# Squaring the queries and keys behind their two rotary products instead of ahead of them

## The chip, the cores and the metric

The kernel runs on one core of one Trainium2 chip. The metric is the device time of one execution in microseconds (us). An engine's name here is the profile's: PE is TensorE (with PEld for its weight loads), DVE is VectorE, ACT is ScalarE, POOL is GpSimd, SP is SyncE, which only issues transfers. SBUF is the on-chip working memory; PSUM is the small memory, in banks of 128 partitions x 512 fp32 numbers, that PE writes its results to and that DVE and ACT read.

## The reference, cut to what matters

The input has 4 sequences of 2048 tokens and 256 channels. A full attention of 16 heads comes first; behind it stand two local layers, and the change lies in these. One local layer computes, for 8 heads of 64:

```python
qkv = h @ wqkv
q, k, v = jnp.split(qkv, 3, axis=-1)
q = l2norm(q) * qs            # t / clip(norm(t), 1e-12), by head
k = l2norm(k) * ksc
q, k = rotary_xpos(q, k)      # q * cos * scale + rotate_half(q) * sin * scale; k with 1 / scale
o = local_attention(q, k, v)  # windows of 128 tokens, each sees itself and the one before
x = x + o @ wo
h = layernorm(shift_token(x)) * lg + lb
a, g = jnp.split(h @ w1 + b1, 2, axis=-1)
x = x + (a * gelu(g)) @ w2 + b2
```

The norm of a query or key is one number by token and head, so it commutes with the rotation. The kernel therefore rotates the raw product and multiplies by the reciprocal norm later.

## The kernel before, in words

The attention comes first and is not touched. The local layers follow: 2 layers x 4 sequences x 16 windows of 128 tokens are 128 steps, each called by its layer, sequence and window (l, b, c). Four steps share one feed-forward block, so the pattern of the work repeats every four steps; c mod 4 names the place in it.

One step runs through these pieces, each on one engine. `project` (from L1408) turns the tokens (`ht`), and `product` (L1434) multiplies them on PE with the three weight tiles into three banks `qkv`, taken from a pool of two banks. For queries (i = 0) and keys (i = 1), `scale` (L1444) reads the finished bank three times: ACT squares it into `sq` (L1454), and DVE multiplies it with two rotary tables into `r` and `t` (L1456). `square_sum` (L1460) sums `sq` by head into `ss` on DVE, and `rotate` (L1465) adds the shifted `t` to `r` on POOL (L1469). `unit` (L1481 to L1491) makes the reciprocal norm: DVE bounds `ss` from below (L380), POOL raises it to the power of minus a half (L381, tile `rn`), DVE scales the eight numbers of the queries (L1487, tile `rn8`) and multiplies the keys by theirs (L1488). For the queries the reciprocal norm enters the exponent later.

`attend` transposes `r` on PE (`qt`, `kt`, L1508), splits each result into a high part on ACT (`lq` L1513, `lk` L1522) and a low part on DVE (L1406, a helper), moves the keys' halves across partitions by DMA (L1528), multiplies (`sim`, L1544), adds the mask and takes the row maximum on DVE (L1556, L1562), exponentiates on ACT (L1570), takes the reciprocal of the sums on DVE (`inv`, L1578) and multiplies by it on POOL (L1581). `gather` transposes these weights on PE (`pT`, L1603), copies them out on ACT and DVE (L1614), weighs the values (`po`, L1624), multiplies with `wo` (`lo`) and adds to the residual (`fg`, L1654). `glu` does the feed-forward block of four steps: the shift by DMA (`shg`), statistics (L391 to L396), normalisation (`hn`, L1689), its transposes (`hnt`, L1704), and the two products, all of whose matmuls stand on L421.

Two things set the order of the work. A timetable written out by hand (`AT`) puts the pieces into slots, and so sets the order in which the instructions are given. A list scheduler then orders each engine's queue by its own estimate of durations and waits. An engine executes its queue strictly in that order. The scheduler also keeps any two engines from touching one PSUM bank at the same time, reads too, in the order in which the two instructions were given: before, DVE's products wait for ACT's square of the same bank.

Of the kernel before, what the change touches and what calls it, by code (L numbers as in the profile page):

```python
# [31 lines left out]
AF = mybir.ActivationFunctionType  # L32
# [160 lines left out]
def encoder_kernel(  # L193
# [22 lines left out]
    nc = tc.nc  # L216
# [161 lines left out]
    def inverse_root(dst, var, least, op):  # L378

        nc.vector.tensor_scalar(var, var, least, None, op)  # L380
        nc.gpsimd.tensor_tensor(dst, var, nhalf[:, : var.shape[1]], ALU.pow)  # L381
# [37 lines left out]
    def dense(*args, **kwargs):  # L419
        for product in dense_products(*args, **kwargs):  # L420
            product()  # L421
# [912 lines left out]
    def local_layers():  # L1334
        with ExitStack() as es:
# [11 lines left out]
            def psum(name):  # L1347

                banks = pq if name.startswith("qkv_") else pp
                return banks.tile([P, 512], F32, tag="ps", name=name)  # L1350
# [23 lines left out]
            def put(at, key, pieces):  # L1374

                assert len(pieces) == len(AT[key]), key
                for slot, piece in zip(AT[key], pieces):
                    tt.put(at + slot, piece)

            def each(f, n):  # L1380
                return [partial(f, i) for i in range(n)]
# [22 lines left out]
            def low(dst, src, h):  # L1404

                nc.vector.tensor_tensor(dst, src, h.bitcast(F32), ALU.subtract)  # L1406


            def project(at, l, b, c):

                name = f"{l}_{b}_{c}"
                s = state[l, b, c] = {}
                m = {}

                def start():
                    m["ht"] = [
                        tp.tile([P, 2, P], F32R, tag=f"ht{i}", name=f"ht{i}_{name}")
                        for i in range(2)
                    ]
                    ps = m["hps"] = psum(f"ht_{name}").rearrange("p (k t) -> p k t", t=P)[:, :2]  # L1420
                    g, i = divmod(c, 4)
                    for k in range(2):
                        src = shs[l, b, g][:, i, :] if k else fgs[l, b, g][:, i, :P]
                        nc.tensor.transpose(ps[:, k], src, ident)
                    m["tb"] = tp.tile([P, 4, LD], F32, tag="tb", name=f"tb_{name}")
                    nc.sync.dma_start(m["tb"], tables[l][:, c])

                put(at, "spread", [
                    start,
                    lambda: nc.scalar.copy(m["ht"][0], m["hps"]),  # L1430
                    lambda: low(m["ht"][1], m["hps"], m["ht"][0]),
                ])

                def product(i):  # L1434
                    wt = ws[l, "qkv"[i]].rearrange("p a (k f) -> p a k f", k=2)
                    ps = m["ps", i] = psum(f"qkv_{name}_{i}")
                    dense(
                        ps,
                        [[m["ht"][a][:, k] for a in range(2)] for k in range(2)],
                        [[wt[:, a, k] for a in range(2)] for k in range(2)],  # L1440
                    )

                put(at, "product", each(product, 3))

                def scale(i):
                    if i == 0:
                        s["r"] = tp.tile([P, 2, LH, LD], F32, tag="r", name=f"r_{name}", bufs=2)
                        m["ss"] = small.tile([P, 2 * LH], F32, tag="ss", name=f"ss_{name}")
                    sq = m["sq", i] = tp.tile(
                        [P, LH, LD], F32, tag="sq", name=f"sq_{name}_{i}", bufs=1  # L1450
                    )
                    t = m["t", i] = tp.tile([P, LH, LD], F32, tag="t", name=f"t_{name}_{i}", bufs=1)
                    src = m["ps", i].rearrange("p (h d) -> p h d", h=LH)
                    nc.scalar.activation(sq, src, AF.Square)  # L1454
                    for dst, n in ((s["r"][:, i], 2 * i), (t, 2 * i + 1)):
                        nc.vector.tensor_tensor(  # L1456
                            dst, src, m["tb"][:, n : n + 1, :].to_broadcast([P, LH, LD]), ALU.mult
                        )

                def square_sum(i):  # L1460
                    nc.vector.tensor_reduce(
                        m["ss"][:, i * LH : (i + 1) * LH], m["sq", i], AX.X, ALU.add
                    )

                def rotate(i):  # L1465
                    r4 = s["r"][:, i].rearrange("p h (s d) -> p h s d", s=2)
                    t4 = m["t", i].rearrange("p h (s d) -> p h s d", s=2)
                    for half, op in ((0, ALU.subtract), (1, ALU.add)):
                        nc.gpsimd.tensor_tensor(  # L1469
                            r4[:, :, half, :], r4[:, :, half, :], t4[:, :, 1 - half, :], op  # L1470
                        )

                put(at, "scale", each(scale, 2))
                put(at, "square_sum", each(square_sum, 2))
                put(at, "rotate", each(rotate, 2))

                def copy_v():
                    s["v"] = tp.tile([P, INNER], F32, tag="lv", name=f"lv_{name}", bufs=4)
                    nc.scalar.copy(s["v"], m["ps", 2])

                def root():  # L1481
                    m["rn"] = small.tile([P, 2 * LH], F32, tag="rn", name=f"rn_{name}")
                    inverse_root(m["rn"], m["ss"], 1e-24, ALU.max)

                def unit():
                    s["rn"] = small.tile([P, LH], F32, tag="rn8", name=f"rn8_{name}")
                    nc.vector.tensor_scalar(s["rn"], m["rn"][:, :LH], 8.0, None, ALU.mult)  # L1487
                    nc.vector.tensor_tensor(  # L1488
                        s["r"][:, 1], s["r"][:, 1],
                        m["rn"][:, LH:].unsqueeze(2).to_broadcast([P, LH, LD]), ALU.mult,  # L1490
                    )  # L1491

                put(at, "unit", [copy_v, root, unit])
# [339 lines left out]
            for step, (l, b, c) in enumerate(steps):  # L1833
                at = SLOTS * (step + 1)
                if b == 0 and c == 0:
                    if l:
                        tt.put(at + AT["spread"][0], partial(load, l, ("q", "k", "v")))
                    tt.put(at + AT["turn"][0], partial(load, l, ("wo",)))
                    tt.put(at + AT["stats"][0] - 20, partial(load, l, ("w1", "w2")))
                if c % 4 == 0:  # L1840
                    tt.put(max(0, at + FETCH_AT), partial(fetch, l, b, c // 4))
                project(at, l, b, c)
                attend(at, l, b, c)
                gather(at, l, b, c)
                if c % 4 == 0:
                    glu(at, l, b, c // 4)
# [57 lines left out]
```

## Time and profile before

| what | us |
|---|---|
| median of three executions | 5701.26 (5699.34 to 5702.85) |
| the profiled execution's own time | 5703.29 |
| its span, first to last instruction | 5701.5 |
| first transpose of the local layers (L1424) at | 3034.5 |
| PE busy in 3034 to 5668 (2634 us) | 2477.2 |
| DVE busy there | 2165.9 |
| ACT busy there | 1781.3 |
| POOL busy there | 1644.7 |
| granted PE clock there | 0.99 |

The 128 steps take 2634 us, 20.6 us each. Matmuls overlap in the pipeline, so the busy time of PE overstates its work; how often it really stands still is read from the idle time before an instruction, which the profile gives with the instruction that ended it ("releaser"), and from the distance between starts. A line of the timeline has the start in us, the duration in us, the engine, the line of the kernel, the operation, the tiles as out<-in with their form, the count, and in square brackets the idle time of the engine ahead of it and its releaser.

### The profile page before, as it was taken

What the parts mean: (1) busy time and instruction counts of PE and PEld (TensorE: products, weight loads), DVE (VectorE), ACT (ScalarE), POOL (GpSimd) and SP (SyncE); (2) the same over time, 40 slices, a digit from 0 to 9 for tenths busy, and PEclk for the clock granted to TensorE, in tenths of its full rate; (3) what the DMA queues carried; (4) which work ended last, traced back from release to release, by engine and by line L of the source; (5) the groups of instructions that cost most, each with busy time, mean ns of one, the idle gap of its engine ahead of it and who ended that gap; (6) DMA issues with size and microseconds to landing.
All of it is one profiled execution on the core that took longest, in us unless ns stands there. A gap on an engine that the chain in (4) does not pass through costs nothing.

```text
span 5701.5 us, 107577 instructions
## 1 busy us (share of the span) xinstructions
PE 5435.7 (95%) x35544; PEld 3267.1 (57%) x35544; DVE 4837.5 (85%) x13769; ACT 4495.8 (79%) x9400; POOL 2182.2 (38%) x2358
## 2 busy tenths in 40 slices
PE   7999999999999999999997999999999999999998
PEld 4333334333343333433335788788877887878887
DVE  7888889888899888998885888888887888888886
ACT  4988998989988899999995667666666677667665
POOL 4222112121021211210003666666665666666665
PEclk8999999999999999999998999999999999999999
DMA  4333333333243333332213121222112322222211
GB/s 131 112 105 105 93 101 97 97 97 91 81 140 98 105 95 87 109 95 75 87 43 118 49 55 50 55 55 55 51 52 78 89 56 63 61 62 55 63 52 41
DMA packets 348762, 456.55 MB, mean 80 GB/s; under 512 B 88400, under 2 KB 212304, under 8 KB 346672
## 3 DMA queue, kind: packets, MB, share of 16 engines
q1 hardware_dynamic: 336688, 416.10, 26.1%
q0 software_dynamic: 11520, 33.58, 2.0%
q8 instruction: 285, 4.67, 0.3%
q14 instruction: 269, 2.20, 0.1%
HBM read 267.41 MB, written 105.12 MB: 65 GB/s over the span
## 4 chain that ended last, share of the span: by engine, by line
PE 45%; DVE 20%; ACT 10%; POOL 5%; issue 3%; DMA 1%; POOLq 0%; DVEq 0%; ACTq 0%; SPq 0%
PE acc L1010 11%; PE s L899 10%; PE s L985 7%; PE w L421 4%; ACT sim L1570 4%; PE sim L1544 3%; POOL rn L381 3%; PE qkv L421 3%; DVE lk L1406 2%; PE po L1624 2%; DVE sim L1556 2%; DVE hn L1689 2%; DVE s L913 2%; DVE lq L1406 1%; ACT lk L1522 1%
## 5 line engine op out<-in xcount | busy, mean ns | idle before, releaser
L1000 ACT ACTIVATE e<-s 128x512 f32<-128x512 f32 x4096 | 2216.5, 608 | 169.0 <-DVE s L996 88.8
L899 PE MATMUL s<-k,q 64*128 64x512 f32 x3200 | 1133.5, 458 | 21.4 <-DVE tops L913 11.1
L913 DVE CUSTOM_DVE_ANT_0 s<-s,wide 128x512 f32<-128x512 f32 x1408 | 975.4, 693 | 170.8 <-PE s L899 146.9
L1010 PE MATMUL acc<-e,v 128*32 128x512 f32 x8192 | 1096.4, 605 | 3.0 <-ACT e L1000 2.5
L985 PE MATMUL s<-q,k 64*128 64x512 f32 x4096 | 875.3, 443 | 53.0 <-ACT e L1000 38.7
L1570 ACT ACTIVATE sim<-sim,top,rn 128x256 f32<-128x256 f32 (+1 forms) x1024 | 597.2, 586 | 258.2 <-DVE top L1562 257.7
L899 PEld LDWEIGHTS s<-k,q 64*128 64x128 f32 x3200 | 503.6, 185 | 318.7 <-ACT more L920 132.2
L911 DVE TENSOR_REDUCE tops<-s 128x1 f32<-128x512 f32 x896 | 607.6, 684 | 67.3 <-PE s L899 58.4
L1581 POOL TENSOR_TENSOR sim<-sim,inv 128x512 f32<-128x512 f32 (+1 forms) x512 | 513.5, 1025 | 346.9 <-DVE inv L1578 346.9
L985 PEld LDWEIGHTS s<-q,k 64*128 64x128 f32 x4096 | 431.0, 184 | 356.4 <-ACT e L1000 234.4
L925 DVE CUSTOM_DVE_ANT_0 more<-s,more 128x512 f32<-128x512 f32 x896 | 605.1, 675 | 0.0
L899 PEld LDWEIGHTS s<-kd,q 64*128 64x128 f32 x896 | 164.5, 184 | 739.3 <-DVE tops L913 212.6
L920 ACT ACTIVATE more<-s 128x512 f32<-128x512 f32 x896 | 540.6, 604 | 59.3 <-PE s L899 43.8
L421 PE MATMUL w<-gt,ww 128*128 128x512 f32 x2112 | 546.4, 397 | 3.5 <-DVE lk L1406 3.1
L996 DVE TENSOR_TENSOR s<-s,band 128x187 f32<-128x187 f32 (+2 forms) x1408 | 481.6, 356 | 79.6 <-PE s L985 75.2
L899 PE MATMUL s<-kd,q 64*128 64x512 f32 x896 | 445.3, 497 | 0.2
L421 PEld LDWEIGHTS w<-gt,ww 128*128 128x128 f32 x2112 | 388.0, 189 | 79.5 <-issue 3.7
L1469 POOL TENSOR_TENSOR r<-r,t 128x256 f32<-128x256 f32 x512 | 367.5, 740 | 150.5 <-DVE t L1456 140.7
L1556 DVE CUSTOM_DVE_ANT_0 sim<-sim,cst 128x256 f32<-128x256 f32 (+1 forms) x1024 | 376.0, 407 | 56.8 <-PE sim L1544 53.7
L381 POOL TENSOR_TENSOR rn<-ss,nhalf 128x16 f32<-128x16 f32 x128 | 372.9, 2913 | 95.2 <-DVE ss L380 92.4
L1544 PE MATMUL sim<-lk,lq 128*128 128x256 f32 (+1 forms) x2048 | 339.7, 295 | 26.5 <-DVE lq L1406 19.4
L1603 PE MATMUL pT<-cst,sim 128*128 128x128 f32 x1984 | 283.2, 279 | 72.8 <-DVE lk L1406 32.9
(197 smaller groups left out, 9456.1 us busy)
## 6 DMA issues: line engine op xcount, KB each, us to landing
lk<-lk SPq DMA_DIRECT2D x256, 256.0 KB
k<-sm SPq DMA_DIRECT2D x638, 64.0 KB
q<-sm SPq DMA_DIRECT2D x632, 64.0 KB
sm<-part SPq DMA_DIRECT2D x112, 256.0 KB
q<-sm SPq DMA_DIRECT2D x128, 128.0 KB
k<-sm SPq DMA_DIRECT2D x512, 32.0 KB
fg<-f SPq DMA_DIRECT2D x32, 512.0 KB
tb<-td SPq DMA_DIRECT2D x128, 128.0 KB
```

Of the source, the lines that this page charges most:

```text
L381: nc.gpsimd.tensor_tensor(dst, var, nhalf[:, : var.shape[1]], ALU.pow)
L421: product()
L899: nc.tensor.matmul(ps, q1[u // 4 % Q_BUFS][rows, u % 4 * P : (u % 4 + 1) * P], keys, start=True, stop=True,)
L911: nc.vector.tensor_reduce(top, ps, AX.X, ALU.max)
L913: nc.vector.tensor_tensor_reduce(ps, ps, prior, 1.0, LOWEST, ALU.add, ALU.max, top)
L920: nc.scalar.activation(more, pairs.pop((u, 1, half)), AF.Relu)
L925: nc.vector.tensor_tensor_reduce(more, ps, more, 1.0, LOWEST, ALU.add, ALU.max, tops[u // NC][:, chunk(u), 2 * half : 2 * half + 1],)
L985: nc.tensor.matmul(ps, k2[s // 4 % Q_BUFS][rows, kc % 4 * P : (kc % 4 + 1) * P], q2[h % 2][rows, j % 2 * QT : (j % 2 + 1) * QT], start=Tru ...
L1000: nc.scalar.activation(e, sums.pop((s, j)), AF.Exp)
L1010: nc.tensor.matmul(acc[32 * j : 32 * j + 32, :], vs[b, kc][:, own * VS : own * VS + 32], es_.pop((s, j)), start=kc == 0, stop=kc == NC - 1,)
L1570: nc.scalar.activation(w, w, AF.Exp, bias=m["top"][:, h : h + 1], scale=s["rn"][:, h : h + 1], accum_out=m["sums"][:, h : h + 1],)
L1581: nc.gpsimd.tensor_tensor(w, w, m["inv"][:, hs].unsqueeze(2).to_broadcast([P, 2, width]), ALU.mult)
```

## The change

The instruction that squares moves behind the two products of the same bank, within one piece:

```diff
                     src = m["ps", i].rearrange("p (h d) -> p h d", h=LH)
-                    nc.scalar.activation(sq, src, AF.Square)
+
                     for dst, n in ((s["r"][:, i], 2 * i), (t, 2 * i + 1)):
                         nc.vector.tensor_tensor(
                             dst, src, m["tb"][:, n : n + 1, :].to_broadcast([P, LH, LD]), ALU.mult
                         )
+                    nc.scalar.activation(sq, src, AF.Square)
```

No instruction is added or removed. Lines below it have a number that is higher by one in the changed kernel (L1454 becomes L1459; L1460 and all that follow, plus one). Since the scheduler works from the order of the instructions and their waits, it gives the queues of all five engines another order from the local layers on; the queues of the attention stay as they were.

## The prediction

> **What bounds the kernel now.** First the head of the page and the stretches: the change touches only the local layers, so their stretch counts.
>
> ```profile
> span 5701.5 us, 107577 instructions
> ...
> 3034.00:5668.00 2634.00, 2477.18 (x17530) 2076.62 (x17528) 2165.94 (x5898) 1781.32 (x4162) 1644.68 (x1482) 0.99 0.23 61
> ```
>
> The columns are stretch, length, busy time of PE, PEld, DVE, ACT and POOL, clock, DMA share and rate. PE leads with 94%, but DVE has 82%. Next, what PE waits for there (us, times, longest):
>
> ```profile
> PE pT L1603 <- DVE lk L1406: 32.9, 68, 1.4
> PE hnt L1704 <- DVE hn L1689: 21.6, 34, 5.5
> PE sim L1544 <- DVE lq L1406: 19.4, 29, 1.6
> PE pT L1603 <- DVE lq L1406: 14.8, 29, 0.5
> PE pT L1603 <- DVE fg L1654: 13.4, 22, 1.1
> ```
>
> PE never waits long, and where it does, DVE is late: five rows, 102.1 us, 3.2 us in each of the 32 groups of four steps. So PE bounds, except at a few places of a group where DVE's queue does. Third, who waits for the two operations concerned:
>
> ```profile
>   DVE r L1456: 118.2, 97
> ...
>   POOL rn L381: 73.7, 64
> ```
>
> The first line belongs to the square (L1454): DVE stood 118.2 us for it. The second belongs to L1487: DVE stood 73.7 us there for POOL's power. Last, one group's timeline, where c mod 4 goes from 1 to 2:
>
> ```profile
> 5181.61 1.55 PE L421 MATMUL qkv<-wq,ht 128*128 128x512 f32 x6
> 5184.38 0.69 DVE L1456 TENSOR_TENSOR r<-qkv,tb 128x512 f32<-128x512 f32 x1 [1.36 <-ACT sq L1454]
> 5191.72 1.08 PE L1603 MATMUL pT<-cst,sim 128*128 128x128 f32 x8 [0.60 <-DVE lk L1406]
> 5193.38 0.17 DVE L380 TENSOR_SCALAR ss<-ss 128x16 f32<-128x16 f32 x1
> 5193.63 2.92 POOL L381 TENSOR_TENSOR rn<-ss,nhalf 128x16 f32<-128x16 f32 x1 [0.65 <-DVE ss L380]
> 5202.43 0.14 DVE L1487 TENSOR_SCALAR rn<-rn 128x8 f32<-128x8 f32 x1
> 5212.35 0.69 DVE L1406 TENSOR_TENSOR lq<-qt,lq 64x512 fp32r<-64x512 f32 x1
> 5213.10 0.96 PE L1544 MATMUL sim<-lk,lq 128*128 128x256 f32 x4 [0.64 <-DVE lq L1406]
> ```
>
> DVE idles 1.36 us for a square that sits behind exponentials on ACT. Then, from L380 at 5193.38 to the second `lq` at 5213.04, DVE has one gap of 0.45 us, and PE ends by waiting for it: for these 20 us DVE is the bound. L1487 is free there, for its 2.92 us power was done at 5196.55.
>
> **The change part by part.** The work stays: 256 squares of 584 ns, 256 products each of 691 and 680 ns, 256 sums of 676 ns. What changes is who waits.
>
> *The wait on the square goes.* `r` now waits for PE's product alone, and the square for DVE's `t`. The bank is held as long as before (0.58 + 0.69 + 0.68 us in either order), so the pool of two banks costs nothing new. This case's row is the 118.2 us, between two readers of one bank. The Trainium skill, "PSUM — Partial Sum Buffer", section "PSUM bank collisions raise a hardware error", states that two engines in one bank at once are an error, reads against reads too, so that software must order them. By that rule the wait only changes sides, and the sum would hold no gain until it is shown that ACT can bear it; by the row alone it would hold 118.2 us.
>
> How much of it reaches PE I take from the timeline. At c mod 4 = 1, `r` can start at 5183.2 instead of 5184.38. In the changed queue the sum follows `t` directly and waits for the square, which ACT reaches behind the seventh exponential (5184.95), so DVE resumes at 5185.45; the second pair of products, `lq` and `lk` follow, `lk` now not behind the second square on ACT (0.6 us less). I place its end at 5190.85 instead of 5191.57, at the time PE gets there (5189.52 plus twelve matmuls of 0.12): the 0.60 us before `pT` is gone. At c mod 4 = 0, `r` now stands ahead of `inv`, in a gap of 1.97 us in which DVE waited for ACT; since DVE then waits for the square, `lk` gains only some 0.45 us (bounds 0 and 1.45, PE's whole loss there). With 31 groups: -14 us.
>
> *A new wait comes.* The built program shows how the scheduler refilled the queues. What stands on DVE between L380 and L1487, costed with the rows' durations, was some 9.8 us at c = 6, 10 and 14; in the changed queue one statistics instruction (0.2 us) is left. For POOL's 2.9 us power this is no cover. In the group above: L380 ends near 5192.3, POOL (behind its `r` at 5192.98) runs the power from 5193.0 to 5195.9, and DVE stands from 5192.5 to 5195.95, 3.4 us. Queued behind it are `res`, two `pT` copies, eight masked maxima, the statistics, `hn` and the next `lk` and `lq`, for which ACT, the transposes and the matmuls of `sim` wait. Of the 3.4 us, 0.7 are the earlier start, 0.45 the gap at `hn` that fills, and some 0.6 are the `ht` and statistics now done ahead of the wait. Counted through: after L1487 and L1488 (0.8 us) the queue stands at 5196.75 before `res`, which before started at 5194.12; from there to the last `lq` it took 18.92 us, less 0.65 (L1487 and L1488) and 0.45, so 17.8: the end is 5214.55 instead of 5213.04. PE, already waiting, loses 1.5 us. Bounds: 0 if ACT's and PE's lateness gives DVE other gaps to fill, 3.4 if none of it is absorbed. There are 23 such groups: +35 us. SP is not the brake: the `shg` transfers are issued behind `fg`, which stays ahead of the wait.
>
> *c = 2.* Here 3.2 us of work cover the power (3.9 before), so only the gain remains: seven groups by -0.8, -6 us (bounds -1.2 and +0.4).
>
> *c = 4 and two of c = 8.* L1487 follows L380 at once where 2.2 us stood between, and the `lq` and `lk` of the step before now wait behind it. From the profiled c = 8: `lk` ended at 4502.67; with the power running to 4503.4 (POOL is behind its `sim`), L1488 and four of 0.7 us, it would end at 4507.0, 4.3 us later. PE needs the banks and the keys from 4505.27 (`pT`), 4506.93 (`sim`). I take 2.0 us (bounds 0, since PE has feed-forward products in this place, and 4.3), nine times: +18 us.
>
> *At c = 0 and 12, and most c = 8*, the cover rises to 3.6 us, so DVE gains about 1 us. PE shows no loss there; I count nothing. If PE has no other work there, it is up to 22 x 1 us.
>
> The sum: -14 + 35 - 6 + 18 = +33 us, on the profiled execution's 5703.29 (span 5701.5 and 1.8 around it): 5736.3. The median of the runs is 2.0 below that execution, so 5734.
>
> **The rivals.**
> 1. *Faster: DVE's freed 118.2 us win.* In 3034 to 5668 PE waited 32.9 + 14.8 + 13.4 = 61.1 us for `lk`, `lq` and `fg` at `pT`, all at c mod 4 = 0 and 1, where the square goes out of the way. If all of it goes and the new stall at c mod 4 = 2 is absorbed, 5701.3 - 61 = 5640; half of it, 5670. The place that decides is L1487 at c = 6, 10, 14: with the other terms at -2, the 23 stalls must cost PE less than 0.1 us each, thus the 3.4 us must shrink below some 2.0. Against it: the power takes 2907 to 2919 ns in all 128 cases, and DVE had no slack there.
> 2. *Nothing: the waits change sides.* ACT is busy 68% and PE 94%; if PE's own work hides both, the time stays at 5701. For it: PE's idle rows are small. Against it: at c mod 4 = 2 PE already waits for DVE's last `lq`.
> 3. *Slower by more: nothing is absorbed.* 23 x 3.4 + 9 x 4.3 - 20 = +97, so 5798. For it: the weights of step c - 1 pass through DVE, ACT, DVE and POOL before PE can transpose them, so a late maximum costs each of them.
> 4. That the change doesn't do what it says: in the built program `r` waits for PE, and the square for DVE, in all steps seen, so this has no chance of its own.
>
> **How the numbers follow.** My forecast gets 0.45, with its own range 5708 (new waits at half their price) to 5770; rival 1 gets 0.32, rival 2 0.13 and rival 3 0.10. The three median runs span 0.06%, and 0.2% (11.4 us) is about what a measurement can tell from no change. So faster 0.32, same 0.13, slower 0.55. The range leaves out a tenth at either end: 5660 (rival 1 beyond two thirds) to 5785 (rival 3 not quite in full).
>
> **What would show it.** In the changed profile DVE's wait for the square before L1456 is gone, and POOL's `rn` as what L1487 waits for rises from 73.7 to about 23 x 3.4 + 9 x 3.1 + 32 x 1.2 = 145 us; ACT's square waits for DVE's `t`, the sum for ACT's square by about 1 us a group. PE's wait for `lk` before `pT` falls by about half, that for `lq` before `sim` rises from 19.4 towards 50. The steps are wrong if L1487 waits as said while PE's rows stay, or if PE's rows shrink altogether. A wait that I have not placed, of ACT's exponentials behind a square that waits for DVE, would make the time longer than the range.

## The result, and the profile after

The changed kernel takes 5766.56 us (median of four executions, 5765.37 to 5767.48), the kernel before 5702.06 in the same comparison: 64.5 us more, a ratio of 1.0111 with a 95% interval from 1.0098 to 1.0124. The forecast was 5734, +33: right in its direction, and half of the size.

The attention ends within a few us of where it did (the first transpose of the local layers starts at 3035.7 us, before at 3034.5); the rest of the difference lies in the local layers. The head of the page and the stretch of these layers in the changed kernel:

```profile
span 5765.7 us, 107637 instructions
...
3034.00:5732.00 2698.00, 2490.12 (x17538) 2091.51 (x17536) 2180.31 (x5896) 1779.39 (x4164) 1654.31 (x1483) 0.98 0.22 59
```

2698 us in place of 2634, at the same clock within 0.01: PE's busy time has grown by 13 us only, so the time went into standing. What DVE waits for there (us, times, longest; lines behind the edit are one higher than before, so L1488 is the scaling `rn8`, L1489 the keys' product):

```profile
DVE rn L1488 <- POOL rn L381: 160.2, 96, 4.3
...
DVE ss L1462 <- ACT sq L1459: 68.4, 77, 1.1
DVE r L1456 <- PE qkv L421: 45.2, 75, 1.9
DVE t L1456 <- POOL r L1470: 41.6, 58, 1.4
```

The 118.2 us for the square are gone from `r`. In their place DVE waits 68.4 us for the square further on, at the sum; 45.2 for PE's product; and 41.6 for POOL, which must have used the one buffer of `t`. The wait for POOL's power has more than doubled, from 73.7. Then PE's waits:

```profile
PE pT L1604 <- DVE lk L1406: 35.4, 61, 2.1
PE hnt L1705 <- DVE hn L1690: 32.3, 33, 5.5
PE lo L421 <- DVE oT L1406: 31.6, 24, 1.4
PE w L421 <- DVE lq L1406: 25.6, 8, 3.2
PE sim L1545 <- DVE res L1820: 19.0, 21, 1.1
PE qkv L421 <- ACT sq L1459: 13.3, 11, 2.4
```

Three of before's rows are all but gone (`sim` for `lq` 19.4, `pT` for `lq` 14.8 and for `fg` 13.4), and four are new: `lo` for `oT`, `w` for `lq`, `sim` for `res`, `qkv` for `sq`. `hnt` for `hn` has grown from 21.6, and none of the moves below takes that back (32.4 us with both). The row `w` for `lq` has eight entries of up to 3.2 us, as many as L1488 has waits of 4.3 us: six at c = 4 and two at c = 8. Here is one of them, step (1, 2, 4), first in the kernel before:

```profile
5063.82 0.60 PE L1508 MATMUL kt<-cst,r 128*128 128x128 f32 x4
...
5065.67 1.41 DVE L1406 TENSOR_TENSOR lk<-kt,lk 64x512 fp32r<-64x512 f32 x2 [0.46 <-ACT lk L1522]
...
5067.11 0.18 DVE L380 TENSOR_SCALAR ss<-ss 128x16 f32<-128x16 f32 x1
5067.28 2.91 PE L421 MATMUL w<-gt,ww 128*128 128x512 f32 x12
...
5070.04 1.91 PE L1603 MATMUL pT<-cst,sim 128*128 128x128 f32 x16
...
5071.70 0.72 PE L1544 MATMUL sim<-lk,lq 128*128 128x256 f32 x4
```

And the same place in the changed kernel:

```profile
5113.87 0.60 PE L1509 MATMUL kt<-cst,r 128*128 128x128 f32 x4
...
5114.13 0.32 DVE L380 TENSOR_SCALAR ss<-ss 128x16 f32<-128x16 f32 x1
...
5114.38 1.43 POOL L1470 TENSOR_TENSOR r<-r,t 128x256 f32<-128x256 f32 x2
...
5115.77 2.91 POOL L381 TENSOR_TENSOR rn<-ss,nhalf 128x16 f32<-128x16 f32 x1
...
5118.71 1.23 DVE L1488 TENSOR_SCALAR rn<-rn 128x8 f32<-128x8 f32 x1 [4.26 <-POOL rn L381]
...
5120.55 1.39 DVE L1406 TENSOR_TENSOR lq<-qt,lq 64x512 fp32r<-64x512 f32 x2
5121.97 1.41 DVE L1406 TENSOR_TENSOR lk<-kt,lk 64x512 fp32r<-64x512 f32 x2
5122.09 1.63 PE L421 MATMUL w<-gt,ww 128*128 128x512 f32 x6 [3.20 <-DVE lq L1406]
...
5126.78 0.90 PE L1545 MATMUL sim<-lk,lq 128*128 128x256 f32 x4
```

From PE's `kt` to its first `sim` it was 7.88 us, now it is 12.91. DVE stands 4.26 us for a power that POOL can only begin behind its own two products, the scaling behind it takes 1.23 us, and the `lq` and `lk` of the step before are queued behind the scaling and the keys' product.

### The profile page after: what moved, and what is told of

Its sections match the earlier page's. It is cut to its first block, busy times and chain, and to the rows that moved or that the text cites. A ratio compares the mean times of both kernels' runs of the same rounds, so it can differ in the third digit from the quotient of the medians.

```text
span 5765.7 us, 107637 instructions
## 1 busy us (share of the span) xinstructions
PE 5448.1 (94%) x35544; PEld 3280.6 (57%) x35544; DVE 4853.2 (84%) x13769; ACT 4493.0 (78%) x9400; POOL 2191.4 (38%) x2358
## 4 chain that ended last, share of the span: by engine, by line
PE 60%; DVE 23%; POOL 8%; ACT 4%; issue 3%; DMA 1%; SPq 0%; POOLq 0%; DVEq 0%; ACTq 0%
PE acc L1010 16%; PE s L899 13%; PE s L985 10%; PE w L421 6%; PE qkv L421 3%; POOL rn L381 3%; PE sim L1545 3%; POOL sim L1582 3%; PE po L1625 2%; DVE sim L1557 2%; DVE s L913 2%; PE pqk L597 2%; DVE lk L1406 2%; PE pT L1604 2%; ACT sim L1571 2%
## 5 line engine op out<-in xcount | busy, mean ns | idle before, releaser
L1041 POOL TENSOR_TENSOR oall<-o,inv 128x256 f32<-128x256 f32 x64 | 39.8, 622 | 817.5 <-DVE inv L1040 792.0
```

## The experiments

Theory 1: the loss is the order of DVE's queue. L1488 and L1489 now stand directly behind L380 at c = 4, 6, 10, 14 (and twice at c = 8), without work to cover the power. Theory 2: the turned dependency itself costs it (the sum late, the bank held until ACT has read it). Theory 3: some other move of the scheduler.

To move single instructions, the queues of the local layers were written out. At the end of `local_layers` a table gives, by engine, the order of its instructions, and each is tied to the one ahead of it, in order of issue alone:

```diff
+            given = nc.cur_bb.bb.instructions[first_local:]
+            for engine in ("PE", "DVE", "Activation", "Pool", "SP"):
+                mine = [i for i in given if i.engine == getattr(mybir.EngineType, engine)]
...
+                for a, c in zip(queue, queue[1:]):
+                    tc.add_manual_dep(mine[c], mine[a].name, mybir.DependencyInfo(
+                        mybir.DependencyClass.NoSync, mybir.DependencyReason.DATA), reason="queue")
```

With this, an experiment's queues are those of its kernel instruction for instruction, but for the moves shown. A difference "to before" is the difference of the medians in one comparison; each is uncertain by some 7 to 10 us to either side, and what "comes back" from one run to another by no less. No run has written queues and nothing else, but the steps that a run doesn't touch show that the writing itself costs nothing: where c = 4 and 8 are moved in the kernel before, the time from one step's `fg` to the next at c = 9, 10, 11 and 13 to 15 differs from that kernel's by 0.02 us in the mean.

### The dependency alone, in the order of before

```diff
 # the changed kernel; `queue` is the table of the kernel before
+                # the squares stay where the scheduler puts them
+                free = {k for k, i in enumerate(mine) if getattr(i, "func", None) == AF.Square}
+                queue = [q for q in queue if q not in free]
```

> The changed dependency (square behind the two products), but every engine's queue in the local layers in the order of the kernel before; only the squares on ACT stand where the scheduler then puts them. Theory 1 (the loss comes from the order of DVE's queue, the power's wait at L1488 above all): the loss is gone, 5690 to 5710 us; DVE's wait for `rn` is back near 74 us, and in place of 118 us for the square stand some 70 to 120 us in which the sum waits for it. Theory 2 (the turned dependency itself costs it, since the sum now waits for ACT's square and the bank is held until ACT has read it): 5750 to 5770, as the changed kernel. In between, 5715 to 5745, both have a part, in proportion.

Measured: 5729.18, 28.4 us above before; between the theories. DVE's wait for `rn` is 72.1 us, that of the sum for the square 82.8. PE's largest row is new:

```profile
PE qkv L421 <- ACT sq L1459: 47.0, 57, 4.0
```

So in the order of before the turned dependency is not a gain but a cost. ACT is now the last reader of the bank, and PE stands until it is done: in 50 of the 57 cases the square starts 0.2 to 0.5 us behind `t` (means of the two squares) and takes 0.6. Some 6 us are lost in the very first step: from its first transpose to its `fg` it takes 78.4 us here, 79.7 in the changed kernel and 72.0 in the kernel before. In the changed kernel's own order the same row is 13.3 us. Where in ACT's queue the scheduler put the squares was not varied, so this run prices the dependency with that placing.

### The nine places c = 4 and 8, in the changed kernel

```diff
 # DVE's queue, step (l, b, 4)
   L380  ss      max
-  L1488 rn8     scale
-  L1489 r       scale keys
   L1406 lq, lq, lk, lk   (step 3)
   L1655 fg
   L1406 ht1     (step 5)
+  L1488 rn8
+  L1489 r
```

> The changed kernel with its own queues, but at the nine places c = 4 and 8 DVE takes L1488 and L1489 behind the `lq`, `lk`, `fg` and `ht` of the step before, as the kernel before did, and not ahead of them. Theory 1: the nine places cost 5.0 us each and not 2.0, so some 40 to 45 us come back: 5720 to 5728. By the forecast's own price (2.0 each) 18 us come back: 5748. Theory 2 and theory 3 (other moves, such as `res` and `oT`, cost it): 5760 to 5768.

Measured: 5722.80, 22.0 above before in place of 64.5: 42.5 us come back, 4.7 for each of the nine. PE's row `w` for `lq` is gone, and from `kt` to `sim` step (1, 2, 4) takes 7.89 us again (5082.06 to 5089.95), 5.0 less than in the changed kernel.

### The 23 places c = 6, 10, 14, in the changed kernel

```diff
 # DVE's queue, step (l, b, 6)
   L380  ss      max
   L391  st
-  L1488 rn8
-  L1489 r
   L1820 res, L1615 pT, pT, L1820 res, L1557 sim, sim, sim
+  L1488 rn8
+  L1489 r
```

> The changed kernel with its own queues, but at the 23 places c = 6, 10 and 14 DVE takes L1488 and L1489 seven instructions later (behind two `res`, two `pT` copies and three masked maxima of the step before, some 3.7 us of work). The forecast's price is 1.5 us each: 35 us come back, 5731. The reading of the changed trace by PE's progress (some 1 us net in these groups, part of it from other moves) gives 10 to 20 us: 5747 to 5757. Theory 2: 5760 to 5768, since no dependency is changed.

Measured: 5726.53, 25.8 above before: 38.7 us come back, 1.7 a place. The forecast's price for these groups holds, and my reading of the changed trace (10 to 20 us) was too low. PE's rows show where they went: `sim` for `res`, 19.0 us, is gone, and

```profile
PE lo L421 <- DVE oT L1406: 12.9, 24, 1.1
```

is what is left of 31.6.

### Both moves

```diff
 # DVE's queue: the moves of the last two runs together
```

> The changed kernel with its own queues, but with both moves of L1488 and L1489 on DVE together (the nine places c = 4 and 8, and the 23 places c = 6, 10 and 14). If these waits are the whole loss and their costs add (5766.6 less 44 and 40), 5682: faster than the kernel before, by about the 20 us that the forecast had put down as gains (-14 and -6). If the costs overlap (one wait hides part of the other), 5695 to 5710. If another cause carries the loss, above 5715.

Measured: 5677.65, 25.1 us below before (ratio 0.9953, 0.9937 to 0.9970). The two prices add: 42.5 + 38.7 = 81.2, together 89.6. The waits at these 32 places carry the whole loss, and without them the changed kernel is faster by about what the forecast had put down as gains.

### The same two instructions moved up in the kernel before

```diff
 # DVE's queue of the kernel before, step (l, b, 4)
   L380  ss      max
+  L1487 rn8
+  L1488 r
   L1406 lq, L1654 fg, L1406 lq, L1406 ht1
-  L1487 rn8
-  L1488 r
```

> The kernel before with its own queues, but at the nine places c = 4 and 8 DVE takes L1487 and L1488 directly behind L380 (one of the nine stood there already). Theory 1: eight places by 5 to 5.5 us, 5741 to 5747. By the forecast's price of 2.0 us: 5718. Theory 2 (the order alone costs little): 5700 to 5710.

Measured: 5721.85, 21.1 above before, 2.6 for each of the eight places: close to the forecast's 2.0 and half of what the same move costs in the changed kernel. In the order of before the two `lk` stand ahead of L380, only `lq` is delayed, and the wait is 3.0 us, not 4.3.

```diff
 # DVE's queue of the kernel before, step (l, b, 6)
   L380  ss      max
+  L1487 rn8
+  L1488 r
   L1406 ht1, L391 st, L1819 res, L1614 pT, pT, and so on to L1689 hn (30 instructions)
-  L1487 rn8
-  L1488 r
```

> The kernel before with its own queues, but at the 23 places c = 6, 10 and 14 DVE takes L1487 and L1488 directly behind L380, with none of the 9.8 us between. The forecast's price of 1.5 us each gives +35: 5736. If the price is that of the run that moved them later in the changed kernel (1.75 each): 5741. If in the order of before DVE has slack there: 5700 to 5715.

Measured: 5796.35, 93.6 above before, 4.1 for each of the 23, over twice the price that the changed kernel pays for the same wait (its DVE wait is 3.0 us here, 2.8 there). PE's largest row:

```profile
PE sim L1544 <- DVE ht L1406: 74.3, 23, 3.2
```

Here `ht` stands behind L380 in the queue, and so behind the wait; in the changed kernel it stands ahead. All expectations on this run were wrong: the price of a wait is not a property of the two instructions moved; what is queued behind them sets it too.

### Which of the delayed operands PE stands for at c = 4

```diff
 # DVE's queue of the changed kernel, step (l, b, 4), eight places; first run
   L380  ss      max
+  L1406 lq, lq
   L1488 rn8
   L1489 r
-  L1406 lq, lq, lk, lk
+  L1406 lk, lk
 # second run: lk, lk ahead, lq, lq behind
```

> The changed kernel with its own queues, but at eight of the nine places c = 4 and 8 (the ninth has no `lq` there) DVE takes the two `lq` of the step before ahead of L1488, and leaves the two `lk` behind it. The step of the forecast under test is that PE has feed-forward products to run at this place. Theory A (PE's products `w` themselves stand, because the PSUM bank they need is held by `qt` until DVE's `lq` has read it): with `lq` first the products run, and 28 to 40 us of the 44 come back, 5727 to 5739. Theory B (PE stands for the keys, `lk`, at `pT` and `sim`): `lk` still ends 3.7 us late in place of 5.1, so about 12 us come back, 5755.

> The counterpart: at the same eight places the two `lk` go ahead of L1488, and the two `lq` stay behind it. In the changed trace the second `lq` ended near 5121.95; here the second `lq` ends near 5121.3, so by theory A (the bank under `lq`) only some 0.7 us a place come back: 5760. By theory B (the keys) 28 to 40 us come back: 5727 to 5739.

Measured: with `lq` first 5764.40, 62.6 above before, so only 1.9 us come back; with `lk` first 5740.32, 38.5 above, 26.0 us back. Theory A, mine, falls; B holds in its direction, though both of its numbers were too high (12 and 28 to 40 us back). The trace with `lq` first shows why:

```profile
5113.56 2.91 PE L421 MATMUL w<-gt,ww 128*128 128x512 f32 x12
...
5116.82 1.41 DVE L1406 TENSOR_TENSOR lk<-kt,lk 64x512 fp32r<-64x512 f32 x2
5117.53 1.44 SPq L1529 DMA_DIRECT2D lk<-lk  x2
...
5118.37 1.52 PE L1604 MATMUL pT<-cst,sim 128*128 128x128 f32 x12 [1.46 <-DVE lk L1406]
...
5121.08 0.47 PE L1545 MATMUL sim<-lk,lq 128*128 128x256 f32 x2 [1.19 <-DMA lk<-lk]
5122.34 0.80 PE L1545 MATMUL sim<-lk,lq 128*128 128x256 f32 x2 [0.79 <-DMA lk<-lk]
```

The products `w` do run at once, as A said, all twelve in 2.91 us. Then PE stands for `lk` at `pT`, and twice more at `sim` for the transfer that moves the keys' halves, which SP can issue only behind `lk`. With `lk` first, `pT` waits for `lq`, and `sim` follows without a transfer to wait for:

```profile
5098.49 1.52 PE L1604 MATMUL pT<-cst,sim 128*128 128x128 f32 x12 [1.44 <-DVE lq L1406]
...
5099.77 0.72 PE L1545 MATMUL sim<-lk,lq 128*128 128x256 f32 x4
```

So the keys are the longer chain: low part, transfer, `sim`. Neither order alone gives back the 42.5 us of the run that puts both ahead.

### A shorter root on POOL

```diff
-    def inverse_root(dst, var, least, op):
+    def inverse_root(dst, var, least, op, power=ALU.pow):
         nc.vector.tensor_scalar(var, var, least, None, op)
-        nc.gpsimd.tensor_tensor(dst, var, nhalf[:, : var.shape[1]], ALU.pow)
+        nc.gpsimd.tensor_tensor(dst, var, nhalf[:, : var.shape[1]], power)
...
-                    inverse_root(m["rn"], m["ss"], 1e-24, ALU.max)
+                    inverse_root(m["rn"], m["ss"], 1e-24, ALU.max, ALU.subtract)
```

> The changed kernel with its own queues, but the local layers' root on POOL (L381 called from L1484) computes a subtraction in place of the power, so the norms are wrong; every instruction and every queue stays, only this one is shorter (2.91 us before; below 0.7 us by the rows of POOL's larger products). If the power's duration is what L1488 waits for: at c = 6, 10, 14 the 2.8 us fall below 0.5, at c = 4 the 4.3 us to about 1.9 (POOL's own products stand ahead of it), and the 1.2 us at c mod 4 = 1 go: 5766 - 24 - 36 - (0 to 30), so 5676 to 5706. If it is L1489's place ahead of `lq` and `lk` and not the wait: above 5735.

> The kernel before with its own queues and the same shorter root (norms wrong in the same way). Its waits for the power (73.7 us, at c mod 4 = 0 and 1) go. By the run with the five lines in the kernel before, 5645 to 5665; if these waits are covered, 5695 to 5702. The difference between this pair shows what is left of the change without the power's wait: about 0 or below if the turned dependency is a gain, 20 to 45 us if it is a cost of its own.

With a subtraction in place of the power the norms are wrong; the two runs only tell what the power's duration costs.

Measured: POOL's instruction takes 0.22 us in place of 2.91. The changed kernel with it takes 5668.61, 33.2 below before; the kernel before with it 5640.26, 61.5 below. With every queue as it was, the duration of the power alone is worth 98 us to the changed kernel and 61.5 to the kernel before. The difference between the two, 36 us, is what the change lost to the power; 28.3 us remain between the pair. An estimated 13 of these still belong to c = 4 and 8, where L1488 waits 1.57 us at eight places behind POOL's other products: from `kt` to `sim` step (1, 2, 4) takes 9.56 us after (5039.25 to 5048.81) and 7.99 before (5030.49 to 5038.48), and eight times 1.57 is 12.6.

### Five lines in the source

```diff
+            pin = []
...
                 def unit():
                     s["rn"] = small.tile([P, LH], F32, tag="rn8", name=f"rn8_{name}")
-                    nc.vector.tensor_scalar(s["rn"], m["rn"][:, :LH], 8.0, None, ALU.mult)
+                    with tc.issue_after(pin[-1]) if pin else nullcontext():
+                        nc.vector.tensor_scalar(s["rn"], m["rn"][:, :LH], 8.0, None, ALU.mult)
...
                         nc.vector.tensor_tensor_reduce(
                             ...
                         )
+                        if h == 0:
+                            pin.append(nc.cur_bb.bb.instructions[-1])
```

This queues L1487 and L1488 on DVE behind the first masked maximum of the step before; the scheduler orders everything else itself. The first run has it in the changed kernel, the second in the kernel before.

> The changed kernel with five lines in the source in place of a written queue: on DVE L1488 and L1489 are queued behind the first masked maximum of the step before, and the scheduler orders the rest anew. Between L380 and L1488 then lie 3.8 to 13 us of DVE's work in all regular steps, so the wait for the power, 160 us before, should fall below 20. If that wait is what costs: 5670 to 5690 (the 20 us under the kernel before, and a part of the 31 waits of 1.2 us at c mod 4 = 1). If the new order costs elsewhere (later keys): 5700 to 5740.

> The kernel before with the same five lines. Here the wait for the power is 73.7 us, 0.7 and 1.2 us at a time at c mod 4 = 0 and 1, and should go. If DVE's waits at these places reach PE: 5680 to 5695. If they are covered: 5697 to 5705. If the turned dependency is worth its 20 us, this stays above the changed kernel with the same lines; if not, the two come out alike.

Measured: in the changed kernel 5669.61, 33.2 below before (ratio 0.9939, 0.9924 to 0.9954), with one wait of 3.0 us for `rn` left among DVE's rows. In the kernel before 5646.50, 56.3 below (ratio 0.9900, 0.9886 to 0.9915), the fastest version with its norms in place. Its waits of DVE:

```profile
DVE r L1458 <- ACT sq L1456: 123.7, 98, 3.9
...
DVE rn L1490 <- POOL rn L381: 3.6, 1, 3.6
```

All of the wait for the square is still there, and the kernel is 56 us faster: these 56 us didn't need the largest of DVE's waits to go, only the smaller one for the power. What the wait for the square itself still costs isn't shown, for no run takes it away without putting others in its place. And with the power covered in both, the turned dependency, with the order that the scheduler makes of it, is not worth 20 us but costs 23.

## Why the prediction was half right

**The wait that comes (c = 6, 10, 14): right.** Forecast +35, measured 38.7 by undoing it. The two are not quite the same: the 1.5 us a place of the forecast already had the earlier start of 0.7 us taken off, and undoing the wait leaves that start in place, so the forecast's price for the wait alone was nearer 2.2 us than the 1.7 measured. DVE's wait was sized at 3.4 us and is 2.8; L1487's total at about 145 us and is 160.2.

**"c = 4 and two of c = 8": the step that failed, in its size.** The forecast took 2.0 us nine times, +18, between 0, "since PE has feed-forward products in this place", and 4.3. Undoing it gives 42.5 us, 4.7 a place (5.0 in the trace of step (1, 2, 4)): the upper bound or a little more. Two things were wrong. The cover does not exist: the twelve products `w` lie at this place before too, and fill the time up to `pT` to the last (5067.28 to 5070.19, `pT` at 5070.04); the run with `lq` first gave PE these products back at once and gained nothing, for the keys and their transfer end last. Work that is already in the path is no cover for a new delay. And the bound of 4.3 counted L1487 as one of the short rows; it takes 1.23 us here (below). The nearest measurement to the 2.0 is the move in the kernel before, 2.6 a place, where `lk` stands ahead of L380: the forecast had the queue right, but its price is about that of a wait with `lq` alone behind it.

**The gains (-14 and -6): right in the sum, not in the cause.** Without the 32 places the changed kernel is 25 us faster than before (interval some 17 to 36), against 20 forecast. But the row named for it, `pT` for `lk`, did not fall by half: 32.9 before, 35.4 after, 33.8 with both moves. What went are `pT` for `lq` and for `fg`. And the gain is not the dependency's own: with the five lines in both kernels, the turned dependency costs 23 us. I read this so, and no run tests it: the wait for the square and the wait for the power lie close together on DVE (in one group of the kernel before 2.02 us for the square at 5063.33 and 0.68 for the power at 5070.31, then 1.19 for the power at 5094.19 and 1.36 for the square at 5103.32), taking away either gives PE the time, and taking away both does not give it twice.

**"The bank is held as long as before", so that the pool of two "costs nothing new": wrong where the order is that of before** (`qkv` for `sq` 47.0 us), small in the changed order (13.3). It is a term that the sum lacked, as is the loss in the first step.

**The rivals.** Rival 1 (the freed 118.2 us win) fell: they came back as 68.4, 45.2 and 41.6 us at the next instructions of the same queue, and the 23 stalls cost PE 1.7 each where less than 0.1 was needed. Rival 2 (the waits change sides) is right on the square's wait, which did only that, but not on the time: in the order of before the turned dependency costs 28 us. Rival 3 (nothing absorbed, +97) is what happens at c = 4, but not at c = 6, where 1.7 of 2.8 us reach PE. What would show the steps: the waits of DVE and ACT came as listed, the sum's for the square at twice its size (68.4 us, 2.1 a group); of PE's rows only the appearance of new waits did, on `oT`, `res` and on `lq` ahead of `w` instead of ahead of `sim`.

**What stays open.** The 23 us between the two kernels with the five lines: PE's rows differ in several small places (`pT` for `lk` 33.2 against 18.3, `qkv` for `sq` 17.2 against none), and no run separates them. And how much of the first experiment's 28 us would go with the squares placed otherwise on ACT; and why `hnt` waits longer in the changed kernel.

## What to carry to other kernels

An edit that only turns a dependency can be worth little by itself and still let a scheduler move everything around it: compare the built queues, and look for instructions that now stand directly behind the producer of a long operation on another engine. The price of such a wait depends on what is queued behind it: waits of 2.7 to 3.0 us for the same power cost 1.7, 2.6, 4.1 and some 4.5 us a place here (the last with `lq` first, by what didn't come back). And work that already fills the path is no cover. Before a large wait is counted as a gain, ask which other wait lies on the same stretch: here the smaller one, 73.7 us, was worth 56 together with the slow scalings described below, and five lines that queue its waiter later beat both kernels.

## What the hardware showed that was not expected

L1487 scales 128 x 8 numbers and takes 0.13 to 0.2 us in 66 of its 128 executions in the kernel before. In 60 it takes 1.2 to 1.3 us, each time beside a product of POOL (`res` or `mid`) that began as the power ended, as here:

```profile
5070.25 1.29 POOL L1809 TENSOR_TENSOR res<-fg,b 128x512 f32<-128x512 f32 x1
5070.31 1.25 DVE L1487 TENSOR_SCALAR rn<-rn 128x8 f32<-128x8 f32 x1 [0.68 <-POOL rn L381]
```

The waiter of POOL's power is released by the same event that frees POOL for its next product, and POOL starts first, by 0.07 us in each of the 60. At c = 6 of the changed kernel no product follows the power, and the scaling takes its short time behind a longer wait:

```profile
5168.74 0.17 DVE L1488 TENSOR_SCALAR rn<-rn 128x8 f32<-128x8 f32 x1 [2.83 <-POOL rn L381]
```

The Trainium skill, "SBUF — State Buffer", section "Who interferes with whom", says that VectorE's scaling by a constant, in its mode with two ports, and GpSimd share a pair of ports, and that whoever issues first keeps it for its whole instruction. The two rows agree: 1.25 us against the product's 1.29. So a wait of 0.7 us for POOL costs DVE nearly 2, and 60 times 1.1 us, 66, lie behind the 73.7 that the waits' row shows. With the five lines in the kernel before, no execution of the scaling is above 0.73 us. What part of the 56 us is this and what part the wait itself was not separated.
